# Graph attention with a hub stage: the first tile of x loaded in 48, 11, 64 and 5 rows, another order of the first products, the second key product at tile 5, two selection jobs per half tile

## The chip, the core and the metric

The kernel runs on one core of one Trainium2 chip. The core has a matrix engine (TensorE, PE in the profile), a vector engine (VectorE, DVE), a scalar engine (ScalarE, ACT), GpSimd (POOL) and SyncE (SP), which here only starts DMAs; ACT and POOL start some too. "SPq" and "ACTq" in the profile are the DMA starts of SP and ACT. The metric is the device time of one execution in microseconds; the number given for a kernel is the median of its runs.

## What is computed

Two layers of graph attention over 2048 nodes, a normalization, a residual and another normalization, for a batch of 8, with 4 heads in the first layer:

```python
mask = graph + eye(N) > 0
h = einsum('bnc,hdc->bhnd', x, Wh)                 # x [8,2048,64], Wh [4,64,64]
out_h = gat(h, mask) + bh                          # softmax(h h^T where mask) h
z = leaky_relu(concat_of_heads(out_h), 0.2)
h2 = einsum('bnk,dk->bnd', z, Wo)
out2 = gat(h2, mask) + bo
return layernorm(x + layernorm(leaky_relu(out2)) * gamma + beta)
```

The adjacency is sparse (a mean share of links of 1/256, falling with the node's number), so that few nodes have many links.

## The kernel before

The first 60 nodes are *hubs*; their rows of the adjacency are handled densely. The other nodes form 153 sets of 13. For every set a short list of neighbours is selected, their rows are gathered from DRAM, and attention runs on the gathered rows. The program has three parts. In the span of the profile they are the **hub stage** (0 to about 136 us), the first layer over the sets (to about 570 us) and the second layer (to the end). Only the hub stage is changed, apart from one group of parameter loads that moves within it.

The order of the work is written out by hand: every engine runs its instructions in the order in which the Python code issues them, and waits in order. Two kinds of resource put waits into that order. Tiles with several buffers make a writer wait for the buffer's last reader: `two(...)` gives one of two PSUM buffers in turn, `raw` has 3 buffers, `a` has 5, the x rows have 10. And the DMAs of SP and ACT share eight completion semaphores, so that each such DMA waits until the one that had its semaphore before, mostly the eighth before it, has landed.

**Head of the hub stage** (lines 477 to 645). `load_x(0)` (L483) loads the first tile of 128 rows of x, in four DMAs on ACT's queue. A tile holds 128 node rows for 4 pairs of batches, and `spans` cuts it where the order of the nodes jumps: tile 0 in 59 and 69 rows, tile 1 in 12, 72 and 44, twice each since two halves of the batch are loaded apart. On SP stand Wh (L497), the hubs' rows of the adjacency `hubraw` (L500), Wo (L501) and then the stream of adjacency pieces. `load_x(1)` puts six DMAs on ACT. `make_powers` (L519) makes constants; its last lines write a table `number` on DVE (L536, L538). `weights` (L540) forms Gram matrices of the heads (`gram`) and transposed weights (`whT`, and `woT` by L553 and L554). `turn_x(0)` (L560, L643) transposes tile 0, `hub_links` (L591, L592) clips the hubs' links, `hub_mask` (L597, L603, L605) spreads them to a mask and `hub_columns` (L635, L637) multiplies the hub columns by `gram`.

**Loop of the hub stage** (L1050): 16 tiles i of 128 nodes, each with two halves t. In a half, `hub_scores` runs 16 matmuls (L650, PE), the masking subtraction (L654, DVE, tile `e`) and the exponential (L657, ACT); `hub_values` of the half before runs 32 matmuls (L668, PE); once per tile the next tile of x is transposed (L560, PE; L643, ACT). I write e(i,t) for the L654 instruction of tile i, half t.

**Adjacency stream and selection.** `load_adj` (L735, L737 on SP; L742, L747 on POOL) loads a piece of 117 adjacency rows and converts it to `a`; two pieces are issued before the loop (`more(2)`) and two per tile. `make_keys` (L784, L788 on PE, L773 on ACT) forms integer keys of neighbour groups: for the first 54 sets in two products, the first after e(3,1) from the adjacency tiles a0 to a2, the second after e(7,1) from a3 to a5. Then a queue `picks` of 38 jobs on DVE selects the best keys: 16 jobs with MAX8 and MATCH_REPLACE (L801, L803), a merge (L812, L814), 16 more, `slots` (L826 to L834, which also makes `index`, the rows to gather) and four jobs that write masks (L843, L845). `some(3)` pops three jobs after every half tile, behind that half's e in DVE's order.

After the last tile, `own_rows` (L880) and the gathers (L872, POOL) start the first layer over the sets; the first transposition of gathered rows is on L560 with the tile `bank`.

## Time and profile before

| what | value |
|---|---|
| median of the three runs | 829.82 us (826.16 to 832.54) |
| span of the profiled execution | 828.9 us; no other time is listed for it |
| PE busy | 725.0 us (87%) |
| DVE busy | 600.8 us (72%) |
| ACT busy | 529.3 us (64%) |
| POOL busy | 449.9 us (54%) |
| mean granted TensorE clock | 0.974 |

How to read it: a row of the timeline is the start in us, the busy time in us, the engine, the line of the kernel, the operation, and the tiles as output<-inputs with their shapes; "x10" means ten merged instructions; the bracket gives how long the engine had been idle and what ended that. A stage's limit is read from who waits for whom inside the stage; an engine that is 87% busy over the span can still stand idle for most of a stage.

### The profile page before, as it was taken

The page shows a single profiled execution, that of the slowest core. Times are in us where ns is not written, and L with a number is a line of the kernel's source. Part 1 is how long each engine was busy: PE and PEld are TensorE (multiplying, and loading weights), DVE is VectorE, ACT ScalarE, POOL GpSimd, SP SyncE. Part 2 cuts the span into 40 slices and gives each one's busy share as a digit, 9 for nine tenths or more (in the row PEclk, how much of TensorE's full clock was granted, in tenths as well). Part 3 has the DMA queues.
Part 4 walks back from the last instruction along what each step waited for, and adds up shares of the span by engine and source line. Part 5 has one row for each costly group of instructions (what it writes and reads, how often), then busy time and mean ns, then how long its engine had stood idle before and what let it go on. Part 6 is the DMA issues. An engine that isn't in the chain of part 4 may idle for free.

```text
span 828.9 us, 40381 instructions
## 1 busy us (share of the span) xinstructions
PE 725.0 (87%) x17262; PEld 615.5 (74%) x17262; DVE 600.8 (72%) x1328; ACT 529.3 (64%) x1131; POOL 449.9 (54%) x620
## 2 busy tenths in 40 slices
PE   1998688889999999999999999998999899989820
PEld 1675457678788889898989889887787688877620
DVE  3446984568778877898767777764347999998883
ACT  0354445556666667667667667773667899988852
POOL 5455356456445455555545555512777777777600
PEclk9999999999999999999999999999999999999975
DMA  4988744343323333454545545532986667766621
GB/s 83 231 225 240 219 156 111 98 121 98 86 71 90 96 90 98 119 144 139 143 120 141 142 139 137 142 114 88 300 245 185 192 170 214 224 201 197 172 54 32
DMA packets 80262, 121.55 MB, mean 147 GB/s; under 512 B 34539, under 2 KB 50751, under 8 KB 80075
## 3 DMA queue, kind: packets, MB, share of 16 engines
q0 software_dynamic: 24752, 65.67, 29.4%
q1 hardware_dynamic: 50973, 52.11, 21.6%
q8 instruction: 138, 2.26, 1.1%
q10 hardware_dynamic: 4350, 1.10, 0.7%
q14 instruction: 49, 0.40, 0.2%
HBM read 116.81 MB, written 18.25 MB: 163 GB/s over the span
## 4 chain that ended last, share of the span: by engine, by line
PE 61%; DVE 13%; DMA 12%; ACT 5%; issue 4%; SPq 3%; POOL 1%; POOLq 0%; DVEq 0%; ACTq 0%
PE s L901 10%; PE o L927 10%; PE bank L560 8%; PE cat L886 6%; DMA raw<-in_adj_dram 4%; PE o L944 4%; PE cat L579 4%; PE cat L961 4%; PE t L560 3%; PE bank L1343 2%; SPq L1461 2%; PE cat L971 2%; PE o L1373 2%; DMA rows<-table,index 2%; DMA out_dram<-y_s 2%
## 5 line engine op out<-in xcount | busy, mean ns | idle before, releaser
L872 POOL DMA_INDIRECT g<-table,index x154 | 162.3, 1054 | 172.8 <-PE o L927 145.5
L872 POOL DMA_INDIRECT rows<-table,index x153 | 161.2, 1053 | 51.8 <-issue 18.6
L566 ACT ACTIVATE z<-cat,bhp 128x208 f32<-128x208 f32 x154 | 58.4, 430 | 101.7 <-PE cat L579 101.7
L906 DVE TENSOR_TENSOR e<-s,mask 128x832 f32<-128x832 f32 x77 | 78.6, 1020 | 28.4 <-PE s L901 27.6
L927 PE MATMUL o<-g,e 128*64 128x65 f32 x2464 | 92.3, 226 | 5.6 <-issue 5.5
L560 PE MATMUL t<-ident,rows 128*128 128x128 f32 x612 | 86.1, 278 | 10.0 <-DMA rows<-table,index 4.7
L560 PE MATMUL bank<-ident,g 128*128 128x128 f32 x616 | 92.3, 273 | 1.5 <-DVE e L1106 1.2
L927 PEld LDWEIGHTS o<-g,e 128*64 128x64 f32 x2464 | 80.1, 138 | 17.1 <-issue 6.9
L901 PE MATMUL s<-y,xTg 64*64 64x52 f32 x4928 | 88.7, 220 | 0.0
L901 PEld LDWEIGHTS s<-y,xTg 64*64 64x64 f32 x4928 | 78.9, 134 | 12.9 <-issue 12.9
L1497 ACT COPY xts<-t 128x512 f32<-128x512 f32 x153 | 82.2, 583 | 7.0 <-PE t L560 6.0
L1235 ACT COPY xTg<-bank 128x512 f32<-128x512 f32 x154 | 82.6, 596 | 2.4 <-PE bank L560 2.4
L560 PEld LDWEIGHTS t<-ident,rows 128*128 128x128 f32 x612 | 66.5, 140 | 23.0 <-issue 9.9
L913 ACT ACTIVATE e<-e,shifts 128x832 f32<-128x832 f32 x77 | 78.4, 1019 | 2.0 <-DVE e L906 2.0
L742 POOL TENSOR_SCALAR a<-raw 117x1024 bf16<-117x1024 int32 x34 | 38.7, 1140 | 71.5 <-DMA raw<-in_adj_dram 49.1
L560 PEld LDWEIGHTS bank<-ident,g 128*128 128x128 f32 x616 | 73.5, 140 | 4.9 <-issue 1.3
L657 ACT ACTIVATE e<-e,shifts 128x960 f32<-128x960 f32 x32 | 35.1, 1096 | 54.7 <-DVE e L654 49.0
L886 PE MATMUL cat<-xo,gram 128*128 128x208 f32 (+1 forms) x304 | 66.3, 341 | 0.8 <-issue 0.8
L951 ACT COPY otb<-o 128x208 f32<-128x208 f32 x154 | 43.8, 335 | 22.0 <-ACT y L892 10.9
L654 DVE TENSOR_TENSOR e<-sh,maskh 128x960 f32<-128x960 f32 x32 | 36.9, 1154 | 26.6 <-PE sh L650 17.2
L935 DVE TENSOR_TENSOR osb<-o,rall 128x512 f32<-128x512 f32 x77 | 53.2, 692 | 2.7
L934 DVE RECIPROCAL rall<-o 64x8 f32<-64x8 f32 x154 | 31.5, 204 | 31.7 <-PE o L927 30.2
(198 smaller groups left out, 1488.0 us busy)
## 6 DMA issues: line engine op xcount, KB each, us to landing
raw<-in_adj_dram SPq DMA_DIRECT2D x34, 432.0 KB
xr_s<-table SPq DMA_DIRECT2D x19, 256.0 KB
table<-x SPq DMA_DIRECT2D x16, 260.0 KB
table<-rowt SPq DMA_DIRECT2D x152, 26.4 KB
out_dram<-y_s SPq DMA_DIRECT2D x152, 24.0 KB
x<-in_x_dram SPq DMA_DIRECT2D x24, 128.0 KB
table<-xb SPq DMA_DIRECT2D x11, 256.0 KB
table<-share SPq DMA_DIRECT2D x10, 256.0 KB
```

Of the source, the lines that this page charges most:

```text
L560: nc.tensor.transpose(tp[:, q * P:(q + 1) * P], rows[:, q, 1:1 + P], ident)
L566: nc.scalar.activation(z[:, hp], cat[:, :, hp * n:(hp + 1) * n], AF.Identity, bias=bhp[:, hp:hp + 1], scale=1.0)
L872: nc.gpsimd.indirect_dma_start(out=t.rearrange("n q c -> n (q c)"), out_offset=None, in_=table, in_offset=bass.IndirectOffsetOnAxis(ap=ind ...
L886: nc.tensor.matmul(cat[:, k, :n], gram[:, g % 2 * 2 + k, :], held["x", g // 2][:, :n], start=True, stop=True)
L901: nc.tensor.matmul(sp[half(r), p, (q * 2 + j) * M:(q * 2 + j + 1) * M], xt[half(p), j, q, half(r)], y[half(p), (j * Q + q) * M:(j * Q + q ...
L906: nc.vector.tensor_tensor(e[:, :16 * M].rearrange("p (a q n) -> p a q n", a=2, q=Q), sp[:, :, :8 * M].rearrange("p a (q n) -> p a q n", q= ...
L913: nc.scalar.activation(e[:, :16 * M], e[:, :16 * M], AF.Exp, bias=shifts[:, 0:1], scale=1.0)
L927: nc.tensor.matmul(op[half(p), j, o0:o0 + K1], e[:, c0:c0 + 64], rw[j][:, q, sums(p)], start=True, stop=True)
L935: nc.vector.tensor_tensor(osb, v[:, :, :, 1:K1], r.unsqueeze(3).to_broadcast([P, 4, 2, D]), OP.mult)
L951: nc.scalar.copy(ot.rearrange("c h (p w n) -> c p h w n", p=2, w=4)[:, p], v[:, :, p * 64:p * 64 + M].rearrange("c w (n h) -> c h w n", h=H))
L1235: nc.scalar.copy(t[:, k, :], bank[k])
L1497: nc.scalar.copy(xts[pair(s) % 4][:, s % 2, :], tp)
```

## The change

- Tile 0 of x is cut further, at the largest multiple of 16 rows in each run: 48, 11, 64 and 5 rows in place of 59 and 69, so eight DMAs in place of four. They stay on ACT's queue. Tile 1's six DMAs move from ACT to SP, behind Wo and ahead of the adjacency stream.
- The five small parameter loads (bh, bo twice, gamma, beta) move from POOL's start to tile 9 of the loop.
- The first products come in another order: `turn_x(0)`, then `weights`, then `hub_links`, `hub_mask`, `hub_columns`. The table `number` is written after these (`make_numbers`). The product for `woT` leaves `weights` and runs after e(0,1) (`more_weights`).
- The second key product runs after e(5,1) rather than e(7,1), and the selection is queued there.
- `some(2)` pops two jobs per half tile rather than three.

```diff
     def load_x(i):
         t = xrow[i]
+        runs = list(spans(i * P, P))
+        if i == 0:
+            runs = [(at + a, node + a, w) for at, node, n in runs for a, w in ((0, n // 16 * 16), (n // 16 * 16, n % 16))]
         for p in range(2):
-            for at, node, n in spans(i * P, P):
-                (nc.scalar if i < 4 else nc.sync).dma_start(...)
+            for at, node, n in runs:
+                (nc.scalar if i in (0, 2, 3) else nc.sync).dma_start(...)
...
     load_x(1)
-    with nc.allow_non_contiguous_dma(reason="a few hundred bytes of parameters"):
-        nc.gpsimd.dma_start(out=bhp, in_=bh.rearrange("(q e) d -> (e d) q", e=2))
...
+    def load_parameters():
+        with nc.allow_non_contiguous_dma(reason="a few hundred bytes of parameters"):
+            nc.gpsimd.dma_start(out=bhp, in_=bh.rearrange("(q e) d -> (e d) q", e=2))
...
         for row in (0, 32, 64):
             nc.gpsimd.memset(adds[row:row + 1], 1.0)
+
+    def make_numbers():
+        n = HALFN // (SEG // 2)
+        count = held.pop("count")
         for h in range(2):
...
         for r in range(2):
             nc.vector.tensor_copy(gram[half(r), :, half(r)], pw[half(r), r, :H * D].rearrange("c (h e) -> c h e", h=H))
+        for r in range(2):
             nc.scalar.copy(whT[half(r), :], pw[half(r), r, H * D:])
+
+    def more_weights():
         po = two("po")
...
     more(2)
+    turn_x(0)
+    weights()
     hub_links()
-    weights()
-    turn_x(0)
     hub_mask()
     hub_columns()
     load_x(2)
     load_x(3)
+    make_numbers()
...
         if i == 9:
+            load_parameters()
...
-            if t == 1 and i in (3, 7):
-                make_keys(0, (i - 3) // 4, two)
-                if i == 7:
+            if t == 1 and i == 0:
+                more_weights()
+            if t == 1 and i in (3, 5):
+                make_keys(0, (i - 3) // 2, two)
+                if i == 5:
                     picks = pick(0)
...
-            some(3)
+            some(2)
```

Three places show how instructions move. Line numbers of the changed kernel are larger by 3 to 15.

DVE at the head, behind the memsets of the x tiles (`share_87` is the table `number`, `own` the clipped links, `share_90` the product of the hub columns). Before:

```order
L528 MEMSET share_87 128x1024
L536 CAST share_87<-count 1x1024 x2
L538 MEMSET share_87 1x40
L538 MEMSET share_87 1x36
L536 CAST share_87<-count 1x1024 x2
L538 MEMSET share_87 1x41
L538 MEMSET share_87 1x36
L591 TENSOR_SCALAR own<-hubraw_144 60x1024
L591 TENSOR_SCALAR own<-hubraw_145 60x1024
L592 TENSOR_TENSOR own<-own,identb 60x60
L549 COPY gram<-pw 64x4x64 x2
L554 COPY woT<-po 128x128
```

Now:

```order
L533 MEMSET share_87 128x1024
L558 COPY gram<-pw 64x4x64 x2
L603 TENSOR_SCALAR own<-hubraw_148 60x1024
L603 TENSOR_SCALAR own<-hubraw_149 60x1024
L604 TENSOR_TENSOR own<-own,identb 60x60
L615 TENSOR_SCALAR maskh<-pm 128x1920
L649 COPY share_90<-pyh 128x480 x2
L545 CAST share_87<-count 1x1024 x2
L547 MEMSET share_87 1x40
L547 MEMSET share_87 1x36
L545 CAST share_87<-count 1x1024 x2
L547 MEMSET share_87 1x41
```

The casts of `number` went behind the two copies of the hub columns, the copies of `gram` ahead of the links, and the copy of `woT` left the head.

ACT at the start (`x_120` is tile 0 of x, `x_122` tile 1). Before:

```order
L435 ACT_TABLE_LOAD
L483 DMA x_120<-in_x_dram 59x4x64
L483 DMA x_120<-in_x_dram 69x4x64
L483 DMA x_120<-in_x_dram 59x4x64
L483 DMA x_120<-in_x_dram 69x4x64
L483 DMA x_122<-in_x_dram 12x4x64
L483 DMA x_122<-in_x_dram 72x4x64
L483 DMA x_122<-in_x_dram 44x4x64
L483 DMA x_122<-in_x_dram 12x4x64
L483 DMA x_122<-in_x_dram 72x4x64
L483 DMA x_122<-in_x_dram 44x4x64
L550 COPY whT<-pw 64x256 x2
```

Now:

```order
L435 ACT_TABLE_LOAD
L486 DMA x_120<-in_x_dram 48x4x64
L486 DMA x_120<-in_x_dram 11x4x64
L486 DMA x_120<-in_x_dram 64x4x64
L486 DMA x_120<-in_x_dram 5x4x64
L486 DMA x_120<-in_x_dram 48x4x64
L486 DMA x_120<-in_x_dram 11x4x64
L486 DMA x_120<-in_x_dram 64x4x64
L486 DMA x_120<-in_x_dram 5x4x64
L655 COPY xT<-px_251 128x4x128
L560 COPY whT<-pw 64x256 x2
```

The six DMAs of tile 1 left ACT, tile 0 has eight in place of four, and the copy of the transposed tile 0 comes ahead of `whT`.

DVE in the loop, around the start of the selection (`share_85` holds the keys). Before, from e(7,0) on:

```order
L654 TENSOR_TENSOR e_110<-sh_0_993,maskh 128x960
L654 TENSOR_TENSOR e_111<-sh_1_1026,maskh 128x960
L801 MAX share_89<-share_85 128x8
L803 MATCH_REPLACE share_85<-share_89,share_85 128x256
L801 MAX share_89<-share_85 128x8
L803 MATCH_REPLACE share_85<-share_89,share_85 128x256
L801 MAX share_89<-share_85 128x8
L803 MATCH_REPLACE share_85<-share_89,share_85 128x256
L477 MEMSET x_1077 128x4x2
L654 TENSOR_TENSOR e_110<-sh_0_1110,maskh 128x960
```

Now, from e(5,0) on:

```order
L666 TENSOR_TENSOR e_110<-sh_0_808,maskh 128x960
L666 TENSOR_TENSOR e_111<-sh_1_841,maskh 128x960
L813 MAX share_89<-share_85 128x8
L815 MATCH_REPLACE share_85<-share_89,share_85 128x256
L813 MAX share_89<-share_85 128x8
L815 MATCH_REPLACE share_85<-share_89,share_85 128x256
L477 MEMSET x_890 128x4x2
L666 TENSOR_TENSOR e_110<-sh_0_922,maskh 128x960
```

The selection starts behind e(5,1) in place of e(7,1), with two jobs ahead of the next e. Its 38 jobs now end behind e(14,1); before they ended behind e(13,1).

More of the change, by code (lines that the diff above doesn't have):

```diff
@@ L480, in load_x @@
         t = xrow[i]
+        runs = list(spans(i * P, P))
+        if i == 0:
+            runs = [(at + a, node + a, w) for at, node, n in runs for a, w in ((0, n // 16 * 16), (n // 16 * 16, n % 16))]
         for p in range(2):
-            for at, node, n in spans(i * P, P):
-                (nc.scalar if i < 4 else nc.sync).dma_start(out=t[at - i * P:at - i * P + n, :, 1 + p * D:1 + (p + 1) * D],
+            for at, node, n in runs:
+                (nc.scalar if i in (0, 2, 3) else nc.sync).dma_start(out=t[at - i * P:at - i * P + n, :, 1 + p * D:1 + (p + 1) * D],
                                     in_=x[p::2, node:node + n, :].rearrange("q n c -> n q c"))
@@ L502, in fast_kernel @@
     load_x(1)
-    with nc.allow_non_contiguous_dma(reason="a few hundred bytes of parameters"):
-        nc.gpsimd.dma_start(out=bhp, in_=bh.rearrange("(q e) d -> (e d) q", e=2))
-    for k in range(2):
-        nc.gpsimd.dma_start(out=bob[:, k, :], in_=bo.partition_broadcast(P))
-    nc.gpsimd.dma_start(out=gam, in_=gamma.partition_broadcast(P))
-    nc.gpsimd.dma_start(out=bet, in_=beta.partition_broadcast(P))
+    def load_parameters():
+        with nc.allow_non_contiguous_dma(reason="a few hundred bytes of parameters"):
+            nc.gpsimd.dma_start(out=bhp, in_=bh.rearrange("(q e) d -> (e d) q", e=2))
+        for k in range(2):
+            nc.gpsimd.dma_start(out=bob[:, k, :], in_=bo.partition_broadcast(P))
+        nc.gpsimd.dma_start(out=gam, in_=gamma.partition_broadcast(P))
+        nc.gpsimd.dma_start(out=bet, in_=beta.partition_broadcast(P))
     nc.gpsimd.memset(shifts[:, 0:1], -SHIFT1)
@@ L513, in fast_kernel @@
     nc.gpsimd.memset(gram, 0.0)
+    held = {}
     powers = early.tile([120, P], BF16, name="powers")
@@ L525, in make_powers @@
         n = HALFN // (SEG // 2)
-        count = work.tile([P, 2, 512], F32, tag="xTg", name="count", bufs=3).rearrange("p a b -> p (a b)").bitcast(I32)
+        count = held["count"] = work.tile([P, 2, 512], F32, tag="xTg", name="count", bufs=3).rearrange("p a b -> p (a b)").bitcast(I32)
         nc.gpsimd.memset(adds, 0.0)
@@ L856, in fast_kernel @@
     rows = {}
-    held = {}
     LEAD = 9
```

## The prediction

> **What bounds the kernel now.** I read the page first: PE is 87% busy, so the matrix engine bounds the kernel as a whole. The change touches only the first 136 us, so I then read the timeline of that stage, and the busy times of DVE in stretches of it. The head first, up to e(0,0):
>
> ```profile
> 0.78 19.59 ACTq L483 DMA_DIRECT2D x<-in_x_dram  x10
> 6.33 6.50 ACTq L483 DMA_DIRECT2D x<-in_x_dram  x1
> 9.62 1.41 DVE L536 CAST share<-count 1x1024 bf16<-1x1024 int32 x2 [6.83 <-POOL count L529]
> 12.77 0.14 DVE L538 MEMSET share<- 1x41 bf16 x2
> 14.81 0.69 DVE L591 TENSOR_SCALAR own<-hubraw 60x1024 bf16<-60x1024 int32 x1 [1.19 <-DMA hubraw<-in_adj_dram]
> 20.41 0.36 ACT L550 COPY whT<-pw 64x256 f32<-64x256 f32 x1 [18.39 <-DMA x<-in_x_dram]
> 21.61 1.11 PE L560 MATMUL px<-ident,x 128*128 128x128 f32 x4 [5.41 <-DVE woT L554]
> 30.39 1.16 DVE L654 TENSOR_TENSOR e<-sh,maskh 128x960 f32<-128x960 f32 x1 [1.16 <-PE sh L650]
> ```
>
> ACT starts ten DMAs of x in 19.59 us, 1.96 each, since one start alone took 6.50. Its first real work, the copy of whT at 20.41, stands behind them. `gram`, `woT`, the transposition of tile 0 at 21.61 and all that needs them follow, up to e(0,0) at 30.39. The DMA starts set this head; DVE's casts and clips lie under them.
>
> From there to the selection the loop runs at PE's pace; during the selection it runs at DVE's:
>
> ```profile
> 59.98 1.16 DVE L654 TENSOR_TENSOR e<-sh,maskh 128x960 f32<-128x960 f32 x1 [1.49 <-PE sh L650]
> 69.70 1.16 DVE L654 TENSOR_TENSOR e<-sh,maskh 128x960 f32<-128x960 f32 x1 [1.48 <-PE sh L650]
> 70.57 0.82 PE L784 MATMUL pk<-a,powers 117*32 117x512 bf16 x6
> 73.63 0.43 DVE L801 MAX8 share<-share 128x8 f32<-128x256 f32 x1 [2.78 <-ACT share L773]
> 124.01 1.15 DVE L654 TENSOR_TENSOR e<-sh,maskh 128x960 f32<-128x960 f32 x1
> 128.61 1.16 DVE L654 TENSOR_TENSOR e<-sh,maskh 128x960 f32<-128x960 f32 x1 [1.06 <-PE sh L650]
> 131.00 1.16 DVE L654 TENSOR_TENSOR e<-sh,maskh 128x960 f32<-128x960 f32 x1 [1.23 <-ACT e L657]
> ```
>
> These are e(5,1), e(7,1), the second key product, the first job, e(14,0), e(15,0) and e(15,1). The same in stretches (length, DVE busy and its instructions, granted clock, DMA share, GB/s): before the selection, during it, and in the last row L654 alone during it.
>
> ```profile
> 59.98:73.63 13.65, 5.82 (x7) 1.00 0.91 246
> 73.63:124.01 50.38, 46.99 (x122) 0.93 0.65 198
> 73.63:124.01 50.38, 13.76 (x12) 0.93 0.65 198
> ```
>
> In the 13.65 us from e(5,1) to the first job DVE is 43% busy; in the next 50.38 it is 93% busy, with only 12 of the 32 e's. So two tiles pass with DVE half idle, and then DVE holds the loop up.
>
> **The change, part by part.** I cut the span at four rows: e(0,0), e(5,1), the first job, e(15,1). Before: 30.39 + 29.59 + 13.65 + 57.37, and 697.9 behind e(15,1), together 828.9.
>
> *Tile 0 of x.* Eight starts of 48, 11, 64 and 5 rows take the place of four of 59 and 69. No row shows such a piece in isolation. The nearest are Wh's two DMAs, 64 rows of four 256-byte runs, started by SP from 0.74 on: the matrix products that need them begin at 4.80 and 6.35. From above there is the clip at 14.81, which waited for a DMA of the same first microseconds; further still, ACT's own 1.96 us per start (a rival below). A start of 128 rows on SP costs about 0.48:
>
> ```profile
> 0.74 1.44 SPq L497 DMA_DIRECT2D share<-in_L_gnn_Wh_dram  x2
> 4.80 0.47 PE L545 MATMUL pw<-share 64*64 64x64 f32 x2 [4.80 <-DMA share<-in_L_gnn_Wh_dram]
> 6.35 0.49 PE L545 MATMUL pw<-share 64*64 64x64 f32 x4 [0.87 <-DMA share<-in_L_gnn_Wh_dram]
> 7.90 0.42 PE L546 MATMUL pw<-ident,share 64*64 64x64 f32 x2
> 20.69 0.96 SPq L483 DMA_DIRECT2D x<-in_x_dram  x2
> ```
>
> The fourth piece waits for the semaphore of Wh's second DMA (4.8 to 6.35 us); four more starts of 0.48 and a landing of 2 to 3 us make 9, my value, nearer to Wh than to 14.81, because the pieces have Wh's form and at most its rows.
>
> The Trainium skill (DMA: Bandwidth & Descriptors, section "Why a DMA increments its semaphore by 16 and not by 1") says that such a DMA runs on the largest number of engines up to 16 that divides its slowest dimension: 59 rows on one, 69 on three, 48 and 64 on sixteen, 11 and 5 on as many as their rows. The 6.50 against 0.48 per start agrees with it. By that rule the pieces would land like Wh's, and the sum could be 1 to 3 us lower than mine.
>
> *The first products.* From tile 0 at 9.0, by these durations:
>
> ```profile
> 15.42 0.17 DVE L592 TENSOR_TENSOR own<-own,identb 60x60 bf16<-60x60 bf16 x1
> 20.81 0.43 DVE L549 COPY gram<-pw 64x256 f32<-64x256 f32 x1 [4.88 <-ACT whT L550]
> 23.68 2.16 DVE L603 TENSOR_SCALAR maskh<-pm 128x1920 uint8<-128x1920 f32 x1 [2.12 <-PE pm L597]
> 22.66 0.98 PE L597 MATMUL pm<-identb,own 60*128 60x60 bf16 x16
> 25.75 0.65 DVE L637 COPY share<-pyh 128x480 f32<-128x480 f32 x1
> 26.45 2.06 PE L635 MATMUL pyh<-xT,gram 128*128 128x120 f32 x8 [0.82 <-DVE share L637]
> ```
>
> The transposition 1.11; the products of Wh 2.6 (0.6 for the first four, 1.97 from 6.35 to 8.32 for the rest); two copies of gram 0.86; clips 1.55 (0.69 twice and 0.17); mask product 0.98; mask 2.16, with the first hub columns under it on PE; their copy 0.65; the second hub columns 2.06; their copy 0.65; the table `number` 3.3 (9.62 to 12.91 before). With 0.1 at each of the hand-overs that is 25.6 for e(0,0): **4.8 us earlier**. The table now stands on the path; its cover, the wait for ACT, is gone. If tile 0 lands at 6.4 e(0,0) comes at 23.0, if at 14 no gain is left.
>
> *Tiles 0 to 5.* 29.59 as before, and 0.9 for the product of woT, which took 1.1 on a PE just started and now stands behind e(0,1), with its copy of 0.29 on DVE:
>
> ```profile
> 15.09 1.11 PE L553 MATMUL po<-ident,share 64*128 64x64 f32 x4 [6.77 <-DMA share<-in_L_gnn_Wo_dram]
> 21.27 0.29 DVE L554 COPY woT<-po 128x128 f32<-128x128 f32 x1
> ```
>
> So e(5,1) at 56.1. From e(7,1) to the first job it took 3.93; after e(5,1) the same, so the first job at 60.0. It needs the adjacency tile a5, complete at 59.63 before, while the product would now want it at 57.0:
>
> ```profile
> 18.21 1.07 POOL L742 TENSOR_SCALAR a<-raw 117x1024 bf16<-117x1024 int32 x1 [6.03 <-DMA raw<-in_adj_dram]
> 19.31 0.81 SPq L735 DMA_DIRECT2D raw<-in_adj_dram  x1
> 27.62 7.95 DMA raw<-in_adj_dram
> 58.44 1.19 POOL L747 TENSOR_SCALAR_AFFINE_SELECT a<-a 117x5 bf16<-117x5 bf16 x6
> ```
>
> Before, the second piece started at 19.31, behind the first one's conversion at 18.21. Now it waits for the first clip instead (the buffer of hubraw, in the order of the built program), at about 14.4 by the sum above. So the stream runs some 5 us ahead and a5 is there near 55. Tile 1's six DMAs stand ahead of it on SP: 6 x 0.48 = 2.9 us, inside the wait for that clip. I take no stall; if the stream gains nothing, the price is 2.6 us.
>
> *The selection.* Its work is the same: 38 jobs. But 18 e's lie in it in place of 12. 50.38 + 6 x 1.15 = 57.3, so e(15,0) starts at 117.3 and e(15,1), 2.39 later (131.00 - 128.61), at 119.7: **11.3 us earlier** in all, 6.5 of it here and in the two tiles saved. Bounds: if none of DVE's 3.4 us of idle time recurs, 3.4 less; if it grows with the e's, 18/12 of it, 1.7 more. Would DVE wait for PE, with fewer jobs between the e's? The jobs and the rest take 46.99 - 13.76 = 33.2 us for 38, 0.87 each; with two of them a half takes DVE 1.15 + 1.75 = 2.90. PE alone needs (69.70 - 59.98) / 4 = 2.43 per half, and where DVE had nothing else to do it waited 1.06 to 1.49 us between e's (the brackets), less than two jobs. So DVE stays the bound, and I take the middle.
>
> *Edits at nothing.* Parameter loads, 3.1 us of POOL (1.51 to 4.61) at tile 9: POOL has 11.31 us of idle time ahead of 105.02; 3.1 if that cover were gone. The gathers: the first at 128.15, its first use at 136.03, so 7.9 us of slack, of which about 2 go, since tile 15's rows arrive relatively later.
>
> ```profile
> 1.51 0.92 POOL L504 DMA_DIRECT2D bhp<-in_L_gnn_bh_dram  x1 [0.21 <-issue]
> 4.07 0.54 POOL L508 DMA_DIRECT2D bet<-in_L_gnn_beta_dram  x1
> 105.02 2.25 POOL L742 TENSOR_SCALAR a<-raw 117x1024 bf16<-117x1024 int32 x2 [11.31 <-PE pk L784]
> 128.15 1.11 POOL L872 DMA_INDIRECT g<-table,index  x1 [0.17 <-issue]
> 136.03 1.06 PE L560 MATMUL bank<-ident,g 128*128 128x128 f32 x8 [1.24 <-DVE e L1106]
> ```
>
> Behind e(15,1) the order on every engine is as before, so 697.9 stay. Sum: 25.6 + 30.5 + 3.9 + 59.7 + 697.9 = 817.6 for the span. The profiled execution lies 0.9 below the median of 829.82; with that, **818.5**.
>
> **Rivals.**
>
> 1. *The small pieces cost what the large ones cost.* Eight starts at 1.96 end at 16.5, tile 0 lands at 18.5, e(0,0) comes at 35.1: 9.5 us later than in the sum, 828.0, no change. For it: the price per start is the only one that ACT's queue shows here. Against it: the 0.48 of whole 128-row starts. Halfway, with e(0,0) where it was, 823.3.
>
> The Trainium skill (DMA: Bandwidth & Descriptors, section "Anatomy of one DMA — SWDGE (gpsimd) path") gives a fixed cost of about 2 us per DMA, measured there on GpSimd's path; were the eight pieces to pay it one after the other, the result would be as in this rival. SP's two starts in 0.96 us do not agree with such a row.
>
> 2. *The adjacency stream is not earlier.* With a5 at 59.63 the first job comes at 59.63 + 3.06 = 62.7 (70.57 to 73.63 before) and the time is 821.2; 2.9 later, if tile 1's starts delay the stream, 824.1. For it: the DMA engines are at a share of 0.91 while the stream runs, so it may not speed up.
>
> 3. *Slower: the second key product stops PE.* PE takes its instructions in order; a product placed two tiles earlier and waiting for a5 holds every matmul behind it. The point from which this loses is a5 at 68.2, 11.3 us behind the 57.0 at which it is wanted; that is 4.75 us per piece from 16 on, against (59.63 - 18.21) / 11 = 3.77 before. At 5.7, if x and the stream collide, a5 comes at 78.7 and the time is 829.8 + 10.5 = 840. For it: single waits of 7.95; against it: nothing is added to the bytes.
>
> 4. *A lower clock stretches the selection.* PE still waits for DVE there, and the granted clock was 0.93. If the missing 0.07 stretched all of the selection, 57.3 x 0.075 = 4.3 more, 822.8. For it: e's that wait for PE twice in the rows above; against it: 2.43 is far below 2.90.
>
> **How the numbers follow.** The forecast 0.72, its own range 813 to 822; rival 1 0.10 (823.3 or 828.0), rival 2 0.09, rival 3 0.03, rival 4 0.06. The range to 825 leaves out 828.0, rival 3 and what lies below 813: about 0.12. One per cent is 8.3 us, about what a measurement of this kernel tells from no change; it ends at 821.5. Faster: 0.72 without its upper edge, and half of rival 2: 0.74. Slower: rival 3, 0.03, and the same for the rest, 0.23.
>
> **What would show it.** Right: ACT's eight starts over by 8 us; tile 0 transposed at 8 to 11; e(0,0) at 23 to 28; the second key product within 1 us of e(5,1), no wait for POOL; the first job near 60, DVE over 90% busy until e(14,1); e(15,1) near 120; the same time behind it. Wrong: starts of over 1 us each; a PE wait for `a` at tile 5; e's that wait for PE in the selection; or a stretch behind e(15,1) that gave the gain back.

## The result and the profile after

| | before | changed | ratio |
|---|---|---|---|
| median of the runs | 829.06 us (826.16 to 832.54) | 818.60 us (815.71 to 820.04) | 0.9884, 95% interval 0.9846 to 0.9921 |

The forecast was 818.5. The profiled execution of the changed kernel took 815.71 us, its span is 813.9. In this run as in all that follow the time lies about 1.8 us above the span of the same run.

At the four cuts of the prediction (starts of the rows, in us):

| | before | predicted | after |
|---|---|---|---|
| tile 0 transposed | 21.61 | 9.0 | 9.52 |
| e(0,0) | 30.39 | 25.6 | 26.50 |
| e(5,1) | 59.98 | 56.1 | 58.59 |
| first job | 73.63 | 60.0 | 62.53 |
| e(15,0) | 128.61 | 117.3 | 117.99 |
| e(15,1) | 131.00 | 119.7 | 119.86 |
| behind e(15,1) | 697.9 | 697.9 | 694.0 |

The total is right to 0.1 us and e(15,1) to 0.2, but two of the pieces are not: tiles 0 to 5 took 1.6 us more than I gave them, the selection 1.8 less, and the two errors cancelled. So the closeness of the total is luck: the span of the profiled execution, 813.9, lies 3.7 us below the 817.6 of the sum, and the ratio makes the gain 9.6 us (6.5 to 12.8), where 11.3 was forecast. Here is the timeline of the head after, several engines together in order of time:

```profile
0.77 5.95 ACTq L486 DMA_DIRECT2D x<-in_x_dram  x8
9.52 1.09 PE L572 MATMUL px<-ident,x 128*128 128x128 f32 x4 [9.52 <-DMA x<-in_x_dram]
12.68 0.86 DVE L558 COPY gram<-pw 64x256 f32<-64x256 f32 x2 [9.34 <-PE pw L555]
14.65 1.15 POOL L754 TENSOR_SCALAR a<-raw 117x1024 bf16<-117x1024 int32 x1 [7.32 <-DMA raw<-in_adj_dram]
14.78 1.06 DVE L604 TENSOR_TENSOR own<-own,identb 60x60 bf16<-60x60 bf16 x1
21.68 1.88 PE L662 MATMUL sh<-share,xT 64*64 64x240 f32 x16
22.36 2.22 DVE L545 CAST share<-count 1x1024 bf16<-1x1024 int32 x2
22.93 1.11 POOL L754 TENSOR_SCALAR a<-raw 117x1024 bf16<-117x1024 int32 x1 [1.43 <-DMA raw<-in_adj_dram]
24.78 1.38 DVE L545 CAST share<-count 1x1024 bf16<-1x1024 int32 x2
26.50 1.16 DVE L666 TENSOR_TENSOR e<-sh,maskh 128x960 f32<-128x960 f32 x1
27.71 1.88 PE L662 MATMUL sh<-share,xT 64*64 64x240 f32 x16 [3.10 <-DVE e L666]
29.52 2.00 PE L680 MATMUL oh<-x,e 128*64 128x65 f32 x32
31.45 1.11 PE L565 MATMUL po<-ident,share 64*128 64x64 f32 x4
32.49 1.88 PE L662 MATMUL sh<-share,xT 64*64 64x240 f32 x16
34.51 1.16 DVE L666 TENSOR_TENSOR e<-sh,maskh 128x960 f32<-128x960 f32 x1 [1.61 <-PE sh L662]
36.59 1.04 PE L662 MATMUL sh<-share,xT 64*64 64x240 f32 x16
```

The eight starts are over at 6.7 and tile 0 is there at 9.5: 12 us earlier than before. Of these, e(0,0) keeps 3.9, and e(1,0), 34.51 against 36.51, only 2.0. Two things are to be seen. The product for e(0,0) is done at 23.56, and then DVE still writes the table `number` (the casts), in front of e(0,0), though it stood idle for 9.34 us ahead of `gram`. And PE, which waited 3.10 us for that, runs the same product L662 in 1.88 us up to 34.4, from 36.6 on in 1.04.

Before, the same product (L650 there) became fast at nearly the same time, though the loop had begun 3.9 us later:

```profile
31.61 1.88 PE L650 MATMUL sh<-share,xT 64*64 64x240 f32 x16 [0.24 <-DVE e L654]
35.33 1.04 PE L650 MATMUL sh<-share,xT 64*64 64x240 f32 x16
```

So the head came earlier, and the full speed of PE did not.

In the loop and the selection (again several engines; the first row is the end of a5, the next to last two are e(15,0) and e(15,1) behind the first gather):

```profile
53.96 1.22 POOL L759 TENSOR_SCALAR_AFFINE_SELECT a<-a 117x5 bf16<-117x5 bf16 x6
58.59 1.16 DVE L666 TENSOR_TENSOR e<-sh,maskh 128x960 f32<-128x960 f32 x1 [1.48 <-PE sh L662]
59.47 0.82 PE L796 MATMUL pk<-a,powers 117*32 117x512 bf16 x6
62.53 0.43 DVE L813 MAX8 share<-share 128x8 f32<-128x256 f32 x1 [2.78 <-ACT share L785]
116.69 1.11 POOL L883 DMA_INDIRECT g<-table,index  x1
117.99 1.14 DVE L666 TENSOR_TENSOR e<-sh,maskh 128x960 f32<-128x960 f32 x1
119.86 1.16 DVE L666 TENSOR_TENSOR e<-sh,maskh 128x960 f32<-128x960 f32 x1 [0.72 <-PE sh L662]
125.39 1.07 PE L572 MATMUL bank<-ident,g 128*128 128x128 f32 x8 [1.24 <-DVE e L1121]
```

The second key product starts at 59.47 without a wait (a5 was complete at 55.2), and the first job follows 3.94 us behind e(5,1). The stretches of DVE (length, busy time and instructions, granted clock, DMA share, GB/s; the last row is L666 alone):

```profile
58.59:62.53 3.94, 1.16 (x1) 1.00 0.74 229
62.53:117.99 55.46, 51.49 (x130) 0.97 0.75 211
62.53:117.99 55.46, 20.70 (x18) 0.97 0.75 211
```

DVE is 93% busy in the selection as before, with 18 e's in place of 12. Behind e(15,1) nothing is given back that can be told from scatter: seven profiles of kernels with the early key product and two jobs per half tile (this one and six below, without the three of the other chip) need 694.0 to 699.2 from there to the end, 696.3 in the mean; three with three jobs (before and two below) 695.3 to 697.9, mean 696.4. A single profile scatters there by 2.5 us either way, so the difference of 3.9 in the table says nothing.

### The profile page after: what moved, and what is told of

Read it like the earlier page. It is cut to its first block, busy times and chain, and to the rows that moved or that the text cites. A ratio compares the mean times of both kernels' runs of the same rounds, so it can differ in the third digit from the quotient of the medians.

```text
span 813.9 us, 40390 instructions
## 1 busy us (share of the span) xinstructions
PE 723.4 (89%) x17262; PEld 615.7 (76%) x17262; DVE 601.5 (74%) x1328; ACT 528.9 (65%) x1131; POOL 445.7 (55%) x620
## 3 DMA queue, kind: packets, MB, share of 16 engines
HBM read 116.81 MB, written 18.25 MB: 166 GB/s over the span
## 4 chain that ended last, share of the span: by engine, by line
PE 66%; DVE 16%; DMA 6%; ACT 4%; issue 3%; SPq 2%; POOL 1%; DVEq 0%; POOLq 0%; ACTq 0%
PE o L938 10%; PE s L912 10%; PE bank L572 8%; PE cat L897 7%; PE o L955 4%; PE cat L972 4%; PE cat L591 4%; DMA rows<-table,index 3%; PE t L572 3%; PE bank L1358 2%; PE cat L982 2%; PE oh L680 2%; PE sh L662 2%; SPq L1476 2%; DVE e L666 2%
## 5 line engine op out<-in xcount | busy, mean ns | idle before, releaser
L938 PEld LDWEIGHTS o<-g,e 128*64 128x64 f32 x2464 | 80.5, 140 | 12.7 <-issue 2.5
L897 PEld LDWEIGHTS cat<-xo,gram 128*128 128x128 f32 x304 | 53.1, 202 | 1.3 <-issue 0.8
```

The lines of the kernel that those rows point to most:

```text
L897: nc.tensor.matmul(cat[:, k, :n], gram[:, g % 2 * 2 + k, :], held["x", g // 2][:, :n], start=True, stop=True)
L938: nc.tensor.matmul(op[half(p), j, o0:o0 + K1], e[:, c0:c0 + 64], rw[j][:, q, sums(p)], start=True, stop=True)
```

## The experiments

All twelve runs, with the ratio to runs of the kernel before on the same chip, and rows of each one's profile:

| run | time, us | before, us | ratio, 95% interval | tile 0 | e(0,0) | e(1,0) | e(5,1) | first job | e(15,1) |
|---|---|---|---|---|---|---|---|---|---|
| head_alone | 824.99 | 827.81 | 0.9973 (0.9955 to 0.9991) | 9.53 | 24.77 | 32.77 | 57.30 | 70.96 | 127.45 |
| select_alone | 821.87 | 827.81 | 0.9926 (0.9897 to 0.9954) | 22.20 | 30.98 | 36.02 | 60.27 | 64.20 | 121.33 |
| early_three | 828.97 | 827.81 | 1.0010 (0.9984 to 1.0035) | 21.98 | 30.75 | 35.35 | 58.82 | 62.76 | 131.31 |
| late_two | 823.14 | 827.81 | 0.9951 (0.9932 to 0.9970) | 21.84 | 30.62 | 35.22 | 58.69 | 72.35 | 119.67 |
| x0_primes | 827.96 | 827.96 | 1.0011 (0.9989 to 1.0033) | 20.23 | 36.19 | 42.74 | 66.22 | 70.16 | 128.12 |
| x0_whole | 824.54 | 827.96 | 0.9951 (0.9920 to 0.9982) | 15.59 | 31.71 | 39.03 | 63.25 | 67.19 | 123.96 |
| table_first | 811.41 | 827.96 | 0.9793 (0.9758 to 0.9829) | 9.34 | 22.48 | 27.91 | 51.37 | 55.31 | 112.54 |
| wo_later | 813.62 | 827.96 | 0.9818 (0.9782 to 0.9855) | 9.66 | 25.75 | 32.72 | 57.31 | 61.24 | 120.80 |
| pe_fill | 951.03 | 965.11 | 0.9883 (0.9832 to 0.9934) | 9.48 | 24.72 | 29.91 | 53.38 | 57.32 | 121.11 |
| table_wo | 953.36 | 965.11 | 0.9877 (0.9838 to 0.9916) | 9.44 | 22.30 | 26.90 | 50.37 | 55.67 | 121.34 |
| pe_warm | 951.68 | 965.11 | 0.9879 (0.9826 to 0.9931) | 9.30 | 20.19 | 26.23 | 51.35 | 55.60 | 121.27 |
| jobs_later | 811.78 | 825.70 | 0.9846 (0.9807 to 0.9884) | 9.59 | 23.63 | 29.24 | 52.70 | 58.23 | 114.20 |

Three runs were on a chip on which the kernel before took 965 us too: from about 112 on their profiles show PE standing with nothing released ("issue": 6 to 11% of the chain of waits, 3 to 4% in the other profiles), so that e(15,1) comes 8.8 us behind e(15,0) there, 1.9 in the profile after. Up to there the rows of pe_fill and table_wo look like those of the other chips; pe_warm has two such pauses earlier. For these three the rows of the head count, and the time only as a ratio.

### Which part of the change pays

**head_alone.** The changed kernel with the selection as before:

```diff
-            if t == 1 and i in (3, 5):
-                make_keys(0, (i - 3) // 2, two)
-                if i == 5:
+            if t == 1 and i in (3, 7):
+                make_keys(0, (i - 3) // 4, two)
+                if i == 7:
...
-            some(2)
+            some(3)
```

> The changed head (pieces of tile 0, order of the first products, parameter loads) with the selection as before: second key product after e(7,1), three jobs per half tile. My theory: of the 3.9 us that e(0,0) came earlier in the profile after, only 1.4 were left at e(5,1), and the selection carries them to the end: e(5,1) near 58.6, first job near 72.2, e(15,1) near 129.6, the time 1.4 us below before, 827.7. Rival A, the head is worth its whole 3.9 and the later loss came with the early key product: e(5,1) near 56.1, 825.2. Rival B, the earlier adjacency stream and the moved parameter loads are what carry the gain of the change: e(15,1) under 125, a gain of over 5 us.

Measured: 0.3% faster, 2.2 us (0.7 to 3.7). My 1.4 lies in the interval, rival A's 3.9 and rival B's 5 outside. The rows came 1.2 to 2.2 us earlier than I expected (e(5,1) 57.30 for 58.6, e(15,1) 127.45 for 129.6), but of the 5.6 us at e(0,0) only 2.7 are left at e(5,1). e(0,1) to e(1,0) took 4.85 us again, as in the profile after; the head loses the same there without the early key product. That e(0,0) came 1.7 us earlier than in the profile after, by the same code, is explained under the hardware below.

**select_alone.** The kernel before with the two edits of the selection:

```diff
-            if t == 1 and i in (3, 7):
-                make_keys(0, (i - 3) // 4, two)
-                if i == 7:
+            if t == 1 and i in (3, 5):
+                make_keys(0, (i - 3) // 2, two)
+                if i == 5:
...
-            some(3)
+            some(2)
```

> The head as before; only the second key product after e(5,1) and two jobs per half tile. My theory: a5 is complete at 59.6 here and the product wants it at about 60.9, so PE does not wait; first job near 63.9, 55.5 us of selection as in the profile after, e(15,0) near 119.4, e(15,1) near 121.3, 9.7 us below before: a gain of 9 to 10 us, 819 to 820. Rival A, the changed head is needed so that a5 is there in time: PE waits for POOL at tile 5 and the gain is under 7. Rival B, the gain lies in the head: under 3.

Measured: first job 64.20, e(15,0) 119.47, e(15,1) 121.33, each within 0.3 us of what I expected; the changed head is not needed for a5. The time fell by 6.1 us (3.8 to 8.5), less than the 9.7 at e(15,1): my 9 to 10 was missed. The profile of before that I counted from is of an execution that took about 830.7 us, 2.9 above this chip's median of before; that would make up the difference, but no row shows where the 2.9 lie. The two parts together, 2.2 and 6.1, make 8.3 of the change's 9.6 (0.9884 of 829); their intervals cover the rest.

**early_three.** The kernel before with the key product after e(5,1), still three jobs per half tile (the first of the two hunks above).

> The head as before, the second key product after e(5,1), but three jobs per half tile as before. My theory: DVE is held for 13 half tiles wherever the selection starts; here for those from (5,1) to (11,1), first job near 63.9, the selection over near 114 at e(12,0). The seven half tiles that are left run at PE's pace of about 2.43, so e(15,1) comes near 131 as before: a gain of 0 to 1.5 us. Rival, the earlier start is what brings the gain, since the same 38 jobs are over 9.7 us sooner: e(15,1) near 121.3, a gain of 9 to 10.

Measured: no change, and e(15,1) at 131.31. The stretches of DVE during the selection and behind it, columns as above:

```profile
62.76:110.75 47.99, 45.77 (x122) 0.96 0.68 193
110.75:131.31 20.56, 9.43 (x12) 0.92 0.49 166
```

The same work is over 13 us earlier, and then DVE stands idle for more than half of 20.56 us while PE walks through the last half tiles at its own pace. Starting earlier alone gives nothing.

**late_two.** The kernel before with `some(2)`, the key product still after e(7,1) (the second hunk).

> The head as before, the second key product after e(7,1) as before, but two jobs per half tile. My theory: fewer jobs per half tile is what lets PE run beside DVE: first job at 73.6, then 14 e's at 3.08 each as in the profile after, e(15,0) near 116.8 and e(15,1) near 119.7, as early as in the change. But only 34 of the 38 jobs are out by then: the indices of the gathers are ready only behind e(15,1), near 122, in place of 112 in the profile after, and the gathers start 6 us later than there. So the gain at e(15,1) is 11, and at the end 5 to 10, the rest lost to the wait for the first gathered rows. Rival, the earlier start brings the gain: none here, or a loss, since the selection ends later than before.

Measured: e(15,1) at 119.67, as early as in the change, with the old head and the old start of the selection, though six of the 38 jobs are still to come there. But the time fell by 4.1 us only (2.5 to 5.6), under the 5 to 10 I gave. Its rows around the first gathers, several engines:

```profile
121.94 0.19 DVE L832 TENSOR_SCALAR index<-keysi 128x54 int32<-128x54 int32 x1
122.77 1.11 POOL L872 DMA_INDIRECT g<-table,index  x1 [7.87 <-DVE member L843]
126.24 1.09 PE L560 MATMUL bank<-ident,g 128*128 128x128 f32 x4 [2.09 <-DMA g<-table,index]
133.60 1.02 DVE L906 TENSOR_TENSOR e<-s,mask 128x832 f32<-128x832 f32 x1 [8.43 <-PE s L901]
```

The first gather starts at 122.77 (116.69 in the profile after), PE waits for the gathered rows, and the first weighting of the first layer comes 13.9 us behind e(15,1), where it comes 9.4 behind it in the profile after.

So the two edits do different things. `some(2)` brings e(15,1) forward (select_alone and early_three differ in it alone, and with all 38 jobs ahead of e(15,1) in both they have it at 121.33 and 131.31); the earlier start keeps the indices ahead of the gathers. The price of a half tile says why. With no job in it a half takes 2.43 us (PE), with two jobs 3.08 (55.46 / 18), with three 4.20 (50.38 / 12). Two jobs lie mostly beside PE's work, the third does not. 38 jobs in pairs: 19 halves x 0.65 = 12.4 us lost; in threes: 12.7 x 1.77 = 22.4. The difference of 10 us is the gain at e(15,1), whenever the selection starts.

### Why tile 0 lands so early

**x0_primes.** As many DMAs as in the change, cut at 53, 6, 61 and 8 rows:

```diff
-            runs = [(at + a, node + a, w) for at, node, n in runs for a, w in ((0, n // 16 * 16), (n // 16 * 16, n % 16))]
+            runs = [(at + a, node + a, w) for (at, node, n), c in zip(runs, (53, 61)) for a, w in ((0, c), (c, n - c))]
```

> The changed kernel, but tile 0 of x is cut in 53, 6, 61 and 8 rows: as many DMAs as in the change and nearly the same pieces. The Trainium skill (DMA: Bandwidth & Descriptors, section 'Why a DMA increments its semaphore by 16 and not by 1') has a DMA on the largest number of engines up to 16 that divides its rows: 53 and 61 on one, 48 and 64 on sixteen. My theory, that this number is what counts: the starts on ACT are as slow again as before (over 1 us each, one of several us), tile 0 is transposed at 14 to 20 in place of 9.5 and e(0,0) comes 3 to 9 us later than in the profile after; the time 1 to 5 us above the change. Rival, smaller pieces land earlier whatever their number of rows: tile 0 transposed near 9.5, the same time as the change.

**x0_whole.** The cut taken out, so 59 and 69 rows on ACT's queue as before; tile 1 stays on SP.

```diff
-        if i == 0:
-            runs = [(at + a, node + a, w) for at, node, n in runs for a, w in ((0, n // 16 * 16), (n // 16 * 16, n % 16))]
```

> The changed kernel with tile 0 of x in 59 and 69 rows again, four DMAs. My theory: 59 rows go out one after the other, tile 0 lands at 14 to 19, e(0,0) 3 to 8 us later than in the profile after; the table of numbers is written under the wait only if it stands early, and it does not here; time 1 to 5 us above the change. Rival, tile 0 was late before only because tile 1's six DMAs stood with it on ACT: with those gone it is transposed near 9.5 and nothing changes.

The starts of tile 0 on ACT's queue and its transposition, first with 53, 6, 61 and 8 rows:

```profile
0.78 16.42 ACTq L486 DMA_DIRECT2D x<-in_x_dram  x8
20.23 1.09 PE L572 MATMUL px<-ident,x 128*128 128x128 f32 x4 [20.23 <-DMA x<-in_x_dram]
```

and with 59 and 69 rows:

```profile
0.77 9.60 ACTq L484 DMA_DIRECT2D x<-in_x_dram  x4
15.59 1.08 PE L570 MATMUL px<-ident,x 128*128 128x128 f32 x4 [15.59 <-DMA x<-in_x_dram]
```

Eight pieces nearly as large as those of the change cost 16.42 us to start, where the change's cost 5.95. Both figures run from the first start to the end of the last, waits for semaphores included. The starts of 53 and 61 rows themselves take 0.3 to 0.5 us; the starts of 6 and 8 rows, each behind one of them, take 2.0 to 4.5. Not the size or the number of the pieces counts, but the number of rows. It is not where in the tile a piece begins, either: tile 1's six pieces, which begin at rows 0, 12 and 84, start within 2.92 us in the profile after, on SP:

```profile
6.97 2.92 SPq L486 DMA_DIRECT2D x<-in_x_dram  x6
```

The rival fell, and x0_primes is as slow as before: the selection still gains, but e(0,0) comes 5.8 us later than before. The loss is larger than the 1 to 5 us I expected, about 10 against the change (1.0011 and 0.9884), since the late tile delays everything by 9.7 at e(0,0) and the table of numbers behind it hides nothing. With tile 1 off ACT's queue, 59 and 69 rows still land at 15.6, and the time is 5.5 us above the change (0.9951), so that rival fell too. The Trainium skill (DMA: Bandwidth & Descriptors, section "Why a DMA increments its semaphore by 16 and not by 1") puts 53, 59 and 61 rows on one engine, 69 on three, 48 and 64 on sixteen; the times agree, 16.42 and 9.60 against 5.95; the number of engines itself stands in none of these rows.

### What the head lost again

**table_first.** The changed kernel, with the table written in DVE's idle time:

```diff
     make_powers()
+    make_numbers()
...
     load_x(3)
-    make_numbers()
```

> The changed kernel with the table of numbers written where it stood before, ahead of everything that waits for x, in DVE's idle time from 3.3 to 12.7. My theory: in the profile after, the product for e(0,0) is ready at 23.56, and e(0,0) waits for the table until 26.50; so e(0,0) comes at 23.6, 2.9 earlier, the time 1.5 to 2.9 us below the change (815.7 to 817). Rival, the casts wait for GpSimd's count and then stand in front of gram: nothing gained or a loss of up to 2.

Measured: 811.41 us, ratio 0.9793; its interval ends at 0.9829, below the change's 0.9846. At e(15,1) it is 7.3 us ahead of the change, more than twice the 2.9 that I expected. DVE and PE in its head:

```profile
7.87 1.50 DVE L545 CAST share<-count 1x1024 bf16<-1x1024 int32 x2
23.70 1.43 PE L662 MATMUL sh<-share,xT 64*64 64x240 f32 x16 [0.24 <-DVE e L666]
25.06 1.15 PE L680 MATMUL oh<-x,e 128*64 128x65 f32 x32
26.14 0.66 PE L565 MATMUL po<-ident,share 64*128 64x64 f32 x4
27.91 1.16 DVE L666 TENSOR_TENSOR e<-sh,maskh 128x960 f32<-128x960 f32 x1 [0.78 <-PE sh L662]
```

The casts now end near 9.4 (the second pair starts at 7.87), about where tile 0 lands, and e(0,0) comes 4.0 earlier. From e(0,1) to e(1,0) it takes 2.70 us in place of 4.85: PE waits 0.24 in place of 3.10, and L680 takes 1.15 where it took 2.00, L565 0.66 where it took 1.11. Of the 7.2 us at e(5,1), 4.0 were there at e(0,0), the table's own time and a meeting with POOL that did not recur (see the end); the other 3.2 came behind it, from a PE that became fast 11 us earlier.

**wo_later.** The changed kernel, with the product of woT in the selection:

```diff
-            if t == 1 and i == 0:
+            if t == 1 and i == 7:
                 more_weights()
```

> The changed kernel with the product of woT after e(7,1), in the selection, in place of after e(0,1). My theory: after e(0,1) it runs on a PE that has just started working and holds up e(1,0), part of the 1.9 us that the gain of the head lost between e(0,1) and e(1,0); in the selection PE waits for DVE and it costs only its copy, 0.3. So 1 to 2 us below the change. Rival, the 1.9 us are those of a PE that has not worked for long enough and would be lost there without the product too: e(1,0) 0.5 us earlier at most, the same time.

Measured: e(0,1) to e(1,0) 3.81 us in place of 4.85, so the product is 1.0 of the loss, and the slow PE the rest: between the two theories. In the selection the product costs 0.9 us, not 0.3: e(7,1) to e(8,0) takes 3.79 us, 2.93 in the profile after. So the move gains next to nothing in the rows. The median is 5.0 us below the change's, which no row explains (e(15,1) stands 0.9 later than there, in a profile of the slowest of the four executions), and the two intervals overlap (0.9855 and 0.9846). The time of this run stays unexplained.

**pe_fill.** The changed kernel, with twelve transpositions more that nobody reads:

```diff
     def turn_x(i):
         tp = two(f"px{i}")
         turn(tp[:, 0, :], xrow[i])
+        if i == 1:
+            for _ in range(3):
+                turn(tp[:, 1, :], xrow[0])
```

> The changed kernel with twelve matmuls more: behind the transposition of tile 1 the matrix engine transposes tile 0 three times again, into a half of that PSUM buffer that nobody reads, while it waits for e(0,0) behind the table of numbers (idle 3.10 us in the profile after). My theory: between e(0,1) and e(1,0) the gain of the head shrinks because the matrix engine, which had stood idle for those 3 us, runs at half speed up to 35 (sh 1.88, oh 2.00, where later 1.04 and 1.15); kept busy it is at full speed by the product for e(0,1), so e(0,1) to e(1,0) takes 2.7 to 3.0 in place of 4.85, e(1,0) comes 1.5 to 2.5 us earlier relative to e(0,0), and the time is 1.5 to 2.5 us below the change in spite of the added work. The Trainium skill (TensorE: Matmul & The Clock Gate, section 'Part 1: The HAM clock gate') has half the clock until about 3.4 us of sustained work. Rival, it is the product of woT that stands there (1.11) and the first use of tile 1: e(0,1) to e(1,0) stays at 4.85, and the time at the change's or up to 1 us above.

PE and DVE around the filled wait:

```profile
22.57 2.69 PE L572 MATMUL px<-ident,x 128*128 128x128 f32 x16
24.72 1.16 DVE L669 TENSOR_TENSOR e<-sh,maskh 128x960 f32<-128x960 f32 x1
25.93 1.04 PE L665 MATMUL sh<-share,xT 64*64 64x240 f32 x16 [0.67 <-DVE e L669]
29.91 1.16 DVE L669 TENSOR_TENSOR e<-sh,maskh 128x960 f32<-128x960 f32 x1 [0.78 <-PE sh L665]
```

e(0,1) to e(1,0) takes 2.87 us with the table still on the path and woT's product still there. From e(0,0) to e(1,0) it is 5.2 us, 8.0 in the profile after. More work on PE made this stretch 2.8 us shorter: it is the speed, not the product. The Trainium skill (TensorE: Matmul & The Clock Gate, section "Part 1: The HAM clock gate (the "warmup" mystery)") has half the clock until PE has been busy for some 3.4 us, and again after an idle window; 1.88 and 1.04 for the same product agree with the half. The 3.4 us do not agree with the profile after, where PE was slow for 8.0 us from its restart at 27.71. At e(15,0) pe_fill is 5.6 us ahead of the change (112.34 against 117.99). The gain of time that I expected cannot be seen: the ratio is 0.9883 for the change's 0.9884, on a chip on which all three kernels have e(15,0) at 112.3 to 112.6 and e(15,1) at 121.1 to 121.3, whatever their heads.

**table_wo.** Both edits, table_first and wo_later, at once.

> The table of numbers ahead of what waits for x, and the product of woT after e(7,1): both single edits at once. My theory: with the table gone from the path the matrix engine does not stop before e(0,1) and is at full speed when woT's product comes, so that moving the product is worth only its 0.66 at full speed: e(1,0) 0.6 earlier than with the table alone (27.3 in place of 27.9), e(15,1) near 112, the time 0 to 1 us below that of the table alone (811.4). Rival, the 5.0 us by which the median of the run with woT moved lay below the change are all the product's, and add: 806 to 807.

e(1,0) came at 26.90, 1.0 earlier than with the table alone (I expected 0.6), and e(5,1) at 50.37. But the first job came at 55.67, where it had been at 55.31. PE's second key product shows why:

```profile
52.50 0.38 PE L796 MATMUL pk<-a,powers 117*32 117x512 bf16 x1 [0.65 <-POOL a L759]
53.06 0.38 PE L796 MATMUL pk<-a,powers 117*32 117x512 bf16 x1 [0.18 <-POOL a L759]
```

It waits for a5. With e(5,1) at 50.4 the head has caught up with the adjacency stream in this profile; a still shorter head would gain nothing unless that stream ran faster. And woT's product, in the selection, costs 0.9 there as in wo_later (e(7,1) to e(8,0) 3.78 us, 2.93 in table_first). The time could not be told apart from those of its two neighbours, so whether the single gains add was not decided.

**pe_warm.** Both edits, and throwaway transpositions of the identity ahead of tile 0 and behind the products of Wh:

```diff
+    def warm(n):
+        for k in range(n):
+            nc.tensor.transpose(px0[:, 1, k % 4 * P:(k % 4 + 1) * P], ident, ident)
...
+    px0 = two("px0")
+    warm(34)
     turn_x(0)
     weights()
+    warm(12)
```

> Both edits, and 46 throwaway transpositions of the identity on the matrix engine: 34 ahead of tile 0's transposition, while it waits for x, and 12 behind the products of Wh, while it waits for the clipped links; their output is read by nobody. My theory: the head's products run at half speed because the matrix engine stood idle until 9.3; busy from about 1.5 on it is at full speed when tile 0 lands, so px takes 0.66 in place of 1.08, pm 0.5 in place of 0.98, pyh 1.1 in place of 2.06 and sh 1.04 in place of 1.88; the mask of 2.16 on the vector engine stays. e(0,0) comes 2.5 to 3.5 us earlier than with both edits alone, near 19.5, and the time falls by as much, near 807. Rival, the waits between the products (0.8 to 2.4 us) let the speed fall again: e(0,0) at 22 and no gain; or the 34 run at half speed throughout, 9.3 us, and push tile 0's transposition to 11: a loss of 1 to 2 us.

PE in the head:

```profile
1.36 5.40 PE L571 MATMUL px<-ident 128*128 128x128 f32 x34 [1.36 <-POOL ident masks.py:199]
9.30 0.63 PE L576 MATMUL px<-ident,x 128*128 128x128 f32 x4 [2.54 <-DMA x<-in_x_dram]
16.86 1.15 PE L651 MATMUL pyh<-xT,gram 128*128 128x120 f32 x8 [1.73 <-DVE share L653]
18.25 1.88 PE L666 MATMUL sh<-share,xT 64*64 64x240 f32 x16 [0.24 <-ACT maskh L621]
```

The transposition takes 0.63 and the hub columns 1.15, where they took 1.09 and 2.06, and e(0,0) comes at 20.19, 2.1 earlier than in table_wo (I expected 2.5 to 3.5). Then, at 18.25, the speed falls again, as the rival said. At e(1,0) 0.7 us of it are left. Then PE pauses twice in the middle of a product with nothing released, near 33.5 and 40, and e(5,1) comes 1.0 later than in table_wo; the first job, at 55.60, is where it was. Whether a faster head would gain beyond that was not decided; the time gives no sign of it (0.9879, 0.9877 for table_wo).

### A wait that was no queue

**jobs_later.** table_first, with the selection queued one half tile later:

```diff
-                if i == 5:
-                    picks = pick(0)
...
             some(2)
+            if t == 1 and i == 5:
+                picks = pick(0)
```

> The kernel with the table of numbers first, and one edit more: the first two jobs of the selection are issued behind e(6,0) rather than behind e(5,1). My theory: in that kernel's profile the vector engine, which takes its instructions in order, waits 2.78 us for the keys with e(6,0) queued behind the first two jobs; e(6,0) comes 5.8 us after e(5,1) though the matrix engine needs 2.4 for a half tile. Let past, e(6,0) comes near 54, ahead of the first job at 55.3; the selection still takes the vector engine as long, but one e of it is done before, so e(15,1) comes 1.5 to 2 us earlier, near 110.7 in place of 112.5, and the time is 1 to 2 us below that kernel's 811.4, near 810. Rival, the key product itself holds the matrix engine, and with it e(6,0): e(6,0) not before 56, and nothing gained; or the indices come later by a half tile and the gathers give it back.

PE and DVE behind e(5,1), which stands at 52.70 here:

```profile
55.55 1.04 PE L662 MATMUL sh<-share,xT 64*64 64x240 f32 x16
57.15 1.16 DVE L666 TENSOR_TENSOR e<-sh,maskh 128x960 f32<-128x960 f32 x1 [3.27 <-ACT share L785]
```

My theory fell. With no job ahead of it e(6,0) still came 4.45 us behind e(5,1) (5.81 with the jobs ahead, 2.4 expected), because the key product holds PE for 2 us, so that the product for e(6,0) starts at 55.55, as the rival said. The trace names ACT's copy of the keys as what e(6,0) waited for last; whether it truly needs that copy was not tried. From e(5,1) to e(15,1) it took 61.5 us, 61.2 with the jobs ahead. Nothing was gained: 811.78 us, ratio 0.9846 with an interval that overlaps that of table_first. table_first has the lowest ratio of what was run.

## Why the prediction was right, and where it was not

- **Tile 0.** Right: starts over by 8 (6.7), landing at 9.0 (9.52). Rival 1, that small pieces cost what large ones cost, is settled by x0_primes: pieces of the same size do cost that, with an unlucky number of rows (2.05 us per start, waits included).
- **The first products.** 25.6 was 26.50: 0.5 from the landing, and about 1.5 in the two steps with a DVE instruction that ran beside a POOL conversion (L604 1.06 in place of 0.17, a pair of casts 2.22 in place of 1.38); the products of Wh gave 0.6 back (2.03 for 2.6), and hand-overs that overlapped the other 0.5. "The table now stands on the path; its cover, the wait for ACT, is gone" was right; pricing it at its own 3.3 us was not.
- **Tiles 0 to 5.** This is the term that was mis-sized: "29.59 as before, and 0.9 for the product of woT" took 32.09. The pace of before was that of a PE which became fast at 35.3, 4.9 us behind e(0,0). I had carried it over to a head that starts 3.9 earlier and in which PE stops for 3.10 us ahead of e(0,1); it became fast only at 35.7, 9.2 us behind e(0,0). Taking away the stop (table_first) or filling it (pe_fill) brings the 2 us back; woT's product alone is 1.0 (wo_later).
- **The first job.** Right: 3.94 behind e(5,1), a5 at 55.2 where I had it near 55, no wait. Rivals 2 and 3 did not come about; a wait for a5 appeared only in table_wo, with e(5,1) 8 us earlier, and cost 0.8.
- **The selection.** 57.3 was 55.46. DVE's idle time grew as I allowed (3.97 for 3.4), but the work beside the e's shrank from 33.2 to 30.8: the merge's two copies took 1.0 us in place of 2.1, and one L844 0.19 in place of 1.07 (L832 before). For L832 that is again POOL beside DVE (a conversion starts at 118.28, L832 at 118.34), and chance; what slowed the copies is not shown. Rival 4 took nothing: the granted clock was 0.97.
- **The reason given for the gain.** I read "two tiles pass with DVE half idle" and put the gain on filling them. early_three fills them and gains nothing; late_two leaves them and has e(15,1) at 119.67. The sum came out right because it counted e's and jobs together, but what pays is that two jobs nearly fit beside PE's half tile and three do not; the early start pays only through the indices of the gathers.
- **Edits at nothing.** Right. The parameter loads take 3.1 us of POOL from 85.61 on, with 5.91 idle ahead of its next conversion. The slack of the gathers did not shrink by 2: from the first one at 116.69 to its use at 125.39 it is 8.7 us, 7.9 before.
- **Behind e(15,1).** Unchanged within the scatter, as predicted. The offset of 0.9 between profile and median was not: a time lies about 1.8 above its span, so the profiled execution of before, near 830.7, stood above its median, not below. I had set a span beside a time.

## What to carry to other kernels

A queue of side jobs costs what sticks out beside the bounding engine's step, not what it takes: spread it so thinly that it nearly fits, and start it early enough that its results are not late at the other end. When a wait is removed, look at what had been lying under it: here a table of 3 us came onto the path, and the stop it made kept PE at half speed for 8 us more; moved into idle time, it was worth more than the whole change of the head. And the number of rows of a DMA can matter more than its size or the number of DMAs.

## What the runs showed of the hardware

- **A short DVE instruction beside POOL.** L604 takes 0.18 us alone and took 1.06 where POOL's conversion of 1.15 started just before it (14.65, in the first fence); the casts 1.37 and 2.22. In head_alone, where no conversion met these two, DVE has:

```profile
14.79 0.18 DVE L604 TENSOR_TENSOR own<-own,identb 60x60 bf16<-60x60 bf16 x1
21.49 1.37 DVE L545 CAST share<-count 1x1024 bf16<-1x1024 int32 x2
```

  The two meetings of the profile after cost 0.88 and 0.85 us. L604 takes 1.06 to 1.07 in all three profiles in which a conversion starts 0.10 to 0.14 us ahead of it (this one, x0_whole, jobs_later), and 0.17 to 0.18 in the others. It does not always go against DVE: in head_alone a conversion met the second pair of casts, which kept its 1.38, and took 1.60 itself in place of 1.09. The 0.88 and 0.85 make the 1.7 us between e(0,0) of head_alone and of the change, by the same code. The Trainium skill (GPSIMD Engine Reference, section "1. Specifications") says that the SBUF interface is shared, with contention for DVE instructions that read two SBUF inputs or use both ports; the rows of L604, which reads two tiles, agree; whether the casts use both ports stands in no row. The mechanism itself was not tried.
- **The clock column reads 1.00 where nothing is on record.** In the profile after it reads 1.00 from 10 to 30 us, while L662 takes 1.88 there and 1.04 later. But the trace has no grant on record before 35.7 us. The first record, of the full clock, stands at 35.7 there, at 35.3 in the profile before, at 24.5 in table_first and at 24.1 in pe_fill, in each where the products turn fast. In pe_warm the records begin at 4.4, and there the column shows the slow stretch (length, PE busy and its instructions, granted clock, DMA share, GB/s):

```profile
18.25:25.00 6.75, 6.52 (x68) 0.51 1.04 233
```

  L666 takes 1.88 in it, and 1.04 from 25.05 on. So the slow PE is a granted clock of half; ahead of the first record only the duration of a repeated instruction tells it.
- **How long the speed takes to come, and to go.** From the restart at 27.71 PE worked without a pause and became fast only after 8.0 us. In wo_later, by the same code up to there, the full clock came at 22.7 and was lost again at 26.1, in a stop of 3.57 us. In pe_warm it had the full clock 3.0 us after the first of 34 transpositions (1.36 to 4.4). Those use 128*128 of PE, the products after the restart mostly 64*64 and 128*64; whether that makes the difference was not tried. In pe_warm PE stayed fast over an idle 2.54 us, and fell at 18.1, after a stretch in which it was about 60% busy (47% in its last 3.41 us), with no single pause over 1.73.
